# The recurrence's bias as one bfloat16 matmul, the roots' first guess as three-operand operations, and state weights loaded one stage earlier

## The chip, the cores and the metric

The kernel runs on 1 core of a Trainium2 chip. The metric is the device time of one execution, in microseconds (us); the median of several runs is compared. A core has five engines that run side by side, each through its own list of instructions in a fixed order: TensorE (PE, matmuls, with its weight loads PEld), VectorE (DVE), ScalarE (ACT), GpSimd (POOL) and SyncE (SP, which in this kernel issues most of the DMAs).

## The reference, cut to what matters

Two layers work on x (64 rows of batch × 64 steps × 256 channels) with a condition vector of 64 × 256. Layer 0: a conditioned decay scan, an attention, a modulated linear map, a ternary-weight feed-forward block. Layer 1: a tanh recurrence, a selective state-space block (mamba), a mixture of experts, a second mixture of experts. Each attention and feed-forward part adds to x. The change touches two of these parts and the weights of a third:

```python
# L0 ffn: two bitlinear layers (256 -> 1024 -> 256) with a squared relu between them
def bitlinear(x, norm_w, w):
    v = mean(square(x), axis=-1)                    # per row
    x_norm = x * rsqrt(v + 1e-8) * norm_w
    scale = 127 / clip(max(abs(x_norm), axis=-1), 1e-5)
    x_q = clip(round(x_norm * scale), -128, 127) / scale
    return einsum('bsd,hd->bsh', x_q, ternary(w))
h = act_scale * square(relu(bitlinear(x, norm1_w, w1))) + act_bias
y = bitlinear(h, norm2_w, w2)

# L1 cond: 64 steps, one after the other, on the x that layer 0 leaves
h = tanh(h @ Wh + x_t @ Wx + b)

# L1 attn: mamba, which reads its own weights W_in, W_xproj, W_dt, A_log, ...
```

## The kernel before, in words

**Stages.** One program runs the parts one after the other, with some overlap. By the trace: the conditioned scan (0 to about 152 us), the attention (about 153 to 383), the ternary feed-forward block with the recurrence woven into it (383 to 660), the rest of the recurrence (660 to 677), the head of the mamba block (677 to 722), its loop (to about 1700), and the two mixtures. A scheduler puts each engine's instructions into an order when the kernel is built, from dependences and its own costs, so the order of the source is only roughly that of the engines; no order is written out by hand here except that the matmuls of the recurrence carry a token that keeps them in their own order.

**The feed-forward block** (`ffn0`) works on x transposed, [256 channels, 4096 tokens], in 16 pairs of 256 tokens (`PT` = 4 steps of 64 rows, as `T` = 2 tiles of 128 tokens). A pair passes through nine stages, spread over `depth` = 7 turns, so that a turn of the loop (L726 to L738) does one stage for each of several pairs; 23 turns in all. Per turn:

- `product`: POOL scales x by the condition (L654), PE multiplies (L661), DVE scales the result (L663), ACT takes the sums of squares (L592).
- `weighted`: multiplies by the norm's weights, for 256 channels on POOL (L626), for 1024 on DVE (L628), then DVE finds the largest magnitude (L629).
- `roots_of` (L594 to L614): 1/sqrt(mean + EPS) for the 256-wide norm of one pair and the 1024-wide norm of another, on tiles of 128 × 2 or 128 × 4. DVE forms mean + EPS (L601, two instructions) and a first guess from the bits of the number taken as an integer (L602); then eleven instructions on POOL refine it and form the limit of the scale (L604 to L614).
- `rounded`: DVE inverts the magnitude (L637), takes the lesser of the scale and its limit (L638, which reads what L614 wrote), rounds (L645 on ACT for 1024, L647 on DVE for 256; L649 on DVE for both).
- `turn`, `up`, `turn_back`, `down`: transposes and matmuls on PE (L677, L688, L705, L713, L717), copies and relu on ACT, the square on DVE (L691) and the addition to x on DVE (L719).

**The recurrence** (`rnn`, L761 to L814) is a generator from which each turn from the 7th on takes four steps. Ahead of each four steps, `ahead` puts b + x_t·Wx for the four steps into a PSUM tile: for each of the two halves `o` of the output a bias matmul (L775: a fp32 row of the bias times a row of ones, one partition, 256 columns) and two fp32 matmuls with Wx (L786). Each step is four fp32 matmuls with Wh (L804) and one tanh on ACT (L813), whose result the next step's matmuls read. When the 23 turns are over, the feed-forward block stores x (L740) and the steps that are left run alone.

**The weights of the mamba block** (`mamba_weights`, L817 to L839; ten DMAs on SP) are asked for after the feed-forward block, in the room on chip that its weights leave (L2064 to L2066). A_log is then turned into -exp(A_log) in its own tile (L860 on ACT, L861 on DVE). The head (L892) multiplies the recurrence's output with `Win` (L902, PE) and starts the convolution (L906 on ACT, L909 on DVE).

**Earlier pieces that the change moves.** The scales of the ternary weights need the mean magnitude of w1 and w2 (L517, a DVE reduction over 2048 columns for each); the sums for the modulation use temporaries `ysq`, `wsq`, `d2` (`ffn0_prepared`). These pieces are put beside the conditioned scan and the attention. The conditioned scan works in chunks on DVE and ACT (L94 to L100 in the helper `softplus`, L199, L220).

Of the kernel before, what the change touches and what calls it, by code (L numbers as in the profile page):

```python
# [13 lines left out]
F32 = mybir.dt.float32  # L14
BF16 = mybir.dt.bfloat16
I32 = mybir.dt.int32
AF = mybir.ActivationFunctionType
ALU = mybir.AluOpType
# [3 lines left out]
P = 128  # L22
B, L, D = 64, 64, 256
# [3 lines left out]
KD = D // P  # L27
CB = CH // L
NTT = NT // P
EPS = 1e-8  # L30
# [7 lines left out]
def setup(ctx, tc, a):  # L38

    nc = tc.nc  # L40
    g = SimpleNamespace(nc=nc, tc=tc, a=a)
    const = ctx.enter_context(tc.tile_pool(name="const", bufs=1))
    g.ident = const.tile([P, P], F32, name="ident")
    make_identity(nc, g.ident)
    g.identb = const.tile([P, P], BF16, name="identb")
    make_identity(nc, g.identb)
    g.ones = const.tile([P, 1], F32, name="one")
    nc.vector.memset(g.ones, 1.0)
    g.magic = const.tile([P, 1], F32, name="magic")
    nc.vector.memset(g.magic, MAGIC)  # L50
    g.condT = const.tile([P, KD, B], F32, name="condT")
    nc.sync.dma_start(g.condT, a["condT"].rearrange("(k p) b -> p k b", p=P))
    g.x = tc.dram_tile((D, NT), F32, name="x_mid").rearrange("(k p) t -> p k t", p=P)
    return g
# [476 lines left out]
    return wq, s[:, 0:1], pieces()  # L531


def ffn0_prepared(g, pool, w):

    nc = g.nc
    w.ones = ones = pool.tile([P, P], F32, name="ones")
    nc.gpsimd.memset(ones, 1.0)
    n = KD * w.F // 2
    w.room = room = pool.tile([P, 2 * n], F32, name="room")  # L540
    w.w1q, w.m1, one = ternary(g, pool, w.w1, ones, "w1", room[:, :n])
    w.w2q, w.m2, two = ternary(g, pool, w.w2, ones, "w2", room[:, n:])

    w.ys = ys = pool.tile([P, KD, B], F32, name="ys")
    ysq = pool.tile([P, KD, 2, B], F32, name="ysq")
    wsq = pool.tile([P, KD, D], F32, name="wsq")
    w.d = d = pool.tile([P, D], F32, name="d")
    d2 = pool.tile([P, 2, D], F32, name="d2")

    def squares():  # L550
        nc.vector.tensor_scalar(ys, g.condT, 1.0 / math.sqrt(D), None, ALU.mult)
        for j in range(2):
            nc.vector.tensor_mul(ysq[:, :, j, :], ys, ys)
        nc.vector.tensor_mul(wsq, w.Wc, w.Wc)

    def sums():
        ps = bank(g)
        for k in range(KD):
            nc.tensor.matmul(
                ps[:, :D], ysq[:, k].rearrange("p j b -> p (j b)"), wsq[:, k, :], start=(k == 0), stop=(k == KD - 1)  # L560
            )
        nc.vector.tensor_scalar(d2[:, 0, :], ps[:, :D], EPS, None, ALU.add)

    return chain(one, two, (squares, sums)), (lambda: rsqrt(nc, d2[:, 0, :], d, d2[:, 1, :]),)


def ffn0(g, w, steps):

# [2 lines left out]
    nc, tc = g.nc, g.tc  # L573
# [7 lines left out]
    with (  # L581
# [12 lines left out]
        def roots_of(turn_, which):  # L594


            st = roots[turn_] = p3.tile([P, 4, 2, T], F32, name="roots")
            v, r, y, u = (st[:, i, which, :] for i in range(4))
            ss = sums.pop(turn_)
            for i, n in ((0, D), (1, F))[which]:  # L600
                nc.vector.tensor_scalar(st[:, 0, i, :], ss[:, i, :], 1.0 / n, EPS, ALU.mult, ALU.add)  # L601
            nc.vector.tensor_scalar(r.bitcast(I32), v.bitcast(I32), -0.5, 1597463007.0, ALU.mult, ALU.add)  # L602
            gp = nc.gpsimd
            gp.tensor_mul(y, r, r)  # L604
            gp.tensor_mul(y, y, v)
            gp.tensor_scalar(u, y, 0.375, -1.25, ALU.mult, ALU.add)
            gp.tensor_mul(u, u, y)
            gp.tensor_scalar(u, u, 1.875, None, ALU.add)
            gp.tensor_mul(r, r, u)
            gp.tensor_mul(y, r, r)  # L610
            gp.tensor_mul(y, y, v)
            gp.tensor_scalar(y, y, -0.5, 1.5, ALU.mult, ALU.add)
            gp.tensor_mul(r, r, y)
            gp.tensor_scalar(u, r, 127.0 / 1e-5, None, ALU.mult)  # L614
# [107 lines left out]
        depth = 7  # L722
        pairs = [SimpleNamespace() for _ in range(NP)]
        for turn_ in range(NP + depth):
            which = slice(0 if turn_ < NP else 1, 2 if 0 <= turn_ - 3 < NP else 1)
            if which.start < which.stop:  # L726
                sums[turn_] = p2.tile([P, 2, T], F32, name="ss")
            more = islice(steps, PT if turn_ >= depth else 0)
            for i, (stage, late) in enumerate(stages):
                if i % 2 == 0:  # L730
                    next(more, None)
                p = turn_ - late
                if 0 <= p < NP:
                    stage(p, pairs[p], turn_)
            if which.start < which.stop:
                roots_of(turn_, which)
            for _ in more:
                pass  # L738
# [8 lines left out]
def rnn_weights(g, pool):  # L747
    nc, a = g.nc, g.a
    w = SimpleNamespace()
    w.Wx = pool.tile([P, KD, D], F32, name="Wx")  # L750
    nc.sync.dma_start(w.Wx, a["rnn_Wx"].rearrange("(k p) n -> p k n", p=P))
    w.Wh = pool.tile([P, KD, D], F32, name="Wh")
    nc.sync.dma_start(w.Wh, a["rnn_Wh"].rearrange("(k p) n -> p k n", p=P))
    w.brow = pool.tile([1, D], F32, name="rb")
    nc.sync.dma_start(w.brow, a["rnn_b"].unsqueeze(0))
    w.one = pool.tile([1, 4 * B], F32, name="one")
    nc.vector.memset(w.one, 1.0)
    return w

# [85 lines left out]
def mamba(g, w, hs, beside):  # L845
# [3 lines left out]
    nc, tc = g.nc, g.tc  # L849
    NI, S, R = w.NI, w.S, w.R  # L850
# [4 lines left out]
    PI = 2  # L855
# [1 line left out]
    LEFT = 40  # L857
    BESIDE = 56
    BESIDE_LAST = 72
    nc.scalar.activation(w.A, w.A, AF.Exp)  # L860
    nc.vector.tensor_scalar(w.A, w.A, -1.0, None, ALU.mult)  # L861
    hs2 = hs.rearrange("p k b t -> p k (b t)")
    seq = lambda t: t.rearrange("p (b l) -> p b l", l=L)
    with (
# [3 lines left out]
        tc.tile_pool(name="m5", bufs=5) as p5,  # L868
        tc.tile_pool(name="mps", bufs=1, space=PSUM) as pp,
    ):  # L870
        tags = cycle(("mp", "yp0", "yp1", "cb"))
        one = lambda: pp.tile([P, CH], F32, tag=next(tags), name="mp")
        g.psum, g.tag = pp, "mq"
# [14 lines left out]
        for i in range(3):  # L888
            r = slice(i * 32, i * 32 + S)
# [140 lines left out]
        def decay(s):  # L1030
            c, j = divmod(s, STEPS)
            p, n = divmod(j, S)
            decays[s] = [dAs[(s * PI + i) % len(dAs)] for i in range(PI)]
            for i in range(PI):
                nc.scalar.activation(  # L1035
                    decays[s][i][:, :, 1:],
                    seq(vs[c].delta[p][:, i, :])[:, :, 1:],
                    AF.Exp,
                    scale=w.A[:, p * PI + i, n : n + 1],
                )  # L1040

        for _ in head(0, vs[0]):
# [4 lines left out]
        for s in range(AHEAD):  # L1047
            inputs(s)
        decay(0)
        cb = spread_c(vs[0], 0)  # L1050
        urgent, pieces, others = iter(()), iter(()), iter(())
        mid = None
        for s in range(LAST):
            c, j = divmod(s, STEPS)
            p, n = divmod(j, S)
            now = vs[c]
            if j == 0:
                ahead = head(c + 1, vs[c + 1]) if c + 1 < NCH else iter(())
                pieces = chain(pieces, gates(c, now, 0), islice(ahead, 2 * NI + 1), gates(c, now, PI), ahead)
# [959 lines left out]
def scoped(tc, name, side=None, bufs=1):  # L2019

    stack = ExitStack()
    kw = {"side": side} if side else {}
    return stack.enter_context(tc.tile_pool(name=name, bufs=bufs, **kw)), stack.close
# [3 lines left out]
def tile_adaln_attn_ffn_d2(ctx: ExitStack, tc: tile.TileContext, a: dict, out: bass.AP):  # L2027
    g = setup(ctx, tc, a)
    close_banks = banks(g)
    p_fill, close_fill = scoped(tc, "fill")  # L2030
    p_mid, close_mid = scoped(tc, "w_mid")
    p_x, close_x = scoped(tc, "x")
    p_attn, close_attn = scoped(tc, "w_attn")
    p_raw, close_raw = scoped(tc, "w_raw", side="right")
    w_attn = None

    def loads():
        nonlocal w_attn
        w_scan = scan_weights(g, p_attn)
        w_attn = attention_loads(g, p_attn, p_raw)  # L2040
        residual(g, p_x)
        g.nc.sync.dma_start(w_attn.Wout, a["WoutT"].rearrange("(k p) n -> p k n", p=P))
        return w_scan
# [6 lines left out]
    w_ffn0 = ffn0_weights(g, p_mid)  # L2050
    w_rnn = rnn_weights(g, p_mid)
# [1 line left out]
    weights = packed(g)  # L2053
    p_mix, close_mix = scoped(tc, "w_mix", side="right")
    p_hs, close_hs = scoped(tc, "hs", side="right")
    p_ffn0, close_ffn0 = scoped(tc, "w_ffn0", side="right")
    hs = p_hs.tile([P, KD, B, L], F32, name="hs")
    pieces = ffn0_prepared(g, p_ffn0, w_ffn0)
    spare = hs.rearrange("p k b t -> p (k b t)")
    attention(g, w_attn, cs, pieces, close_banks, spare, w_ffn0.room, w_ffn0.ones)  # L2060
    close_attn()
    with tc.tile_pool(name="steps", bufs=2, space=PSUM) as g.steps, tc.tile_pool(name="psum3", bufs=3, space=PSUM) as g.psum:
        ffn0(g, w_ffn0, rnn(g, w_rnn, hs))
    close_ffn0()  # L2064
    p_mamba, close_mamba = scoped(tc, "w_mamba", side="right")
    w_mamba = mamba_weights(g, p_mamba)  # L2066
    close_x()
    close_mid()
    p_shared, close_shared = scoped(tc, "w_shared", side="right")
# [93 lines left out]
```

## Time and profile before

| what | us |
|---|---|
| runs | 2809.3, 2803.34, 2809.07 |
| median | 2809.07 |
| the profiled execution | 2806.4 |
| its span (first to last instruction) | 2804.7 |
| PE busy in the span | 2368.8 (84%) |
| DVE busy | 1783.4 (64%) |
| ACT busy | 1380.3 (49%) |
| POOL busy | 1323.8 (47%) |

The profiled execution lies 1.7 us above its own span (what lies around it) and 2.7 us below the median of the three runs. The mean granted TensorE clock over the span is 0.924. Lines of the timeline give the start, the duration, the engine, the line of the kernel, the operation, what it writes and reads, and in brackets how long the engine had been idle and what released it. A group's line gives the sum of the busy time, the mean in ns, and the idle time ahead of it. A line of the table of windows gives, for a stretch of time, its length, the busy time of PE, PEld, DVE, ACT and POOL with the count of instructions, the granted clock, the share of the DMA engines, and GB/s.

### The profile page before, as it was taken

The page shows a single profiled execution, that of the slowest core. Times are in us where ns is not written, and L with a number is a line of the kernel's source. Part 1 is how long each engine was busy: PE and PEld are TensorE (multiplying, and loading weights), DVE is VectorE, ACT ScalarE, POOL GpSimd, SP SyncE. Part 2 cuts the span into 40 slices and gives each one's busy share as a digit, 9 for nine tenths or more (in the row PEclk, how much of TensorE's full clock was granted, in tenths as well). Part 3 has the DMA queues.
Part 4 walks back from the last instruction along what each step waited for, and adds up shares of the span by engine and source line. Part 5 has one row for each costly group of instructions (what it writes and reads, how often), then busy time and mean ns, then how long its engine had stood idle before and what let it go on. Part 6 is the DMA issues. An engine that isn't in the chain of part 4 may idle for free.

```text
span 2804.7 us, 34605 instructions
## 1 busy us (share of the span) xinstructions
PE 2368.8 (84%) x12072; PEld 1698.5 (61%) x12092; DVE 1783.4 (64%) x3017; ACT 1380.3 (49%) x2278; POOL 1323.8 (47%) x1158
## 2 busy tenths in 40 slices
PE   3979967998577888888778888869987999999995
PEld 3634435775245555555555555557765778888885
DVE  0467638982699889897978889883354443333332
ACT  0567627783675757676565757543332222222220
POOL 0013336540677676767586878754647341111110
PEclk9879988998768999998899899889999999999997
DMA  9999810002212122212122131314787757555545
GB/s 228 371 359 346 272 45 1 1 1 100 68 61 83 65 73 71 72 65 72 45 71 95 58 102 65 110 42 152 252 269 262 294 202 265 193 194 215 199 167 185
DMA packets 180630, 406.05 MB, mean 145 GB/s; under 512 B 24913, under 2 KB 84562, under 8 KB 175074
## 3 DMA queue, kind: packets, MB, share of 16 engines
q1 hardware_dynamic: 167010, 366.80, 38.7%
q0 software_dynamic: 13440, 36.98, 3.4%
q8 instruction: 97, 1.59, 0.2%
q14 instruction: 83, 0.68, 0.1%
HBM read 280.76 MB, written 144.98 MB: 152 GB/s over the span
## 4 chain that ended last, share of the span: by engine, by line
PE 45%; DVE 25%; issue 8%; ACT 7%; POOL 5%; DMA 3%; SPq 0%; DVEq 0%; POOLq 0%; ACTq 0%
DVE hb L1067 12%; PE ps L1661 11%; PE acc L1559 8%; PE out L446 4%; DVE hb L1069 3%; PE yp L1083 2%; PE mq L1797 2%; PE ps L1628 2%; PE mp L964 2%; DVE xc L909 2%; PE mq L1813 1%; PE acc L437 1%; PE s L412 1%; DVE h L628 1%; PE ps L1669 1%
## 5 line engine op out<-in xcount | busy, mean ns | idle before, releaser
L1028 POOL TENSOR_TENSOR hb<-dx,Bn 128x1024 f32<-128x1024 f32 x256 | 601.3, 2358 | 257.7 <-PE yp L1083 253.3
L1067 DVE TENSOR_TENSOR_SCAN hb<-dA,hb 128x512 f32<-128x512 f32 x512 | 602.5, 1208 | 32.4 <-ACT dA L1035 29.9
L1035 ACT ACTIVATE dA<-delta,A 128x504 f32<-128x504 f32 x512 | 344.4, 683 | 305.3 <-DVE hb L1067 302.7
L1083 PEld LDWEIGHTS yp<-ident,hb 128*128 128x128 f32 x2048 | 272.5, 154 | 179.2 <-issue 141.2
L1069 DVE TENSOR_TENSOR hb<-hb,cb 128x1024 f32<-128x1024 f32 x256 | 312.0, 1219 | 77.0 <-PE cb L980 59.5
L1661 PE MATMUL ps<-gxT,w 128*128 128x256 f32 (+1 forms) x1600 | 324.1, 361 | 0.8 <-DVE gxT L1536 0.8
L1083 PE MATMUL yp<-ident,hb 128*128 128x128 f32 x2048 | 307.6, 295 | 0.0
L1661 PEld LDWEIGHTS ps<-gxT,w 128*128 128x128 f32 x1600 | 276.4, 190 | 46.3 <-issue 12.4
L1797 PE MATMUL mq<-x,moe_s 128*128 128x256 f32 x896 | 254.6, 417 | 47.0 <-ACT up L1804 25.6
L1335 POOL DMA_INDIRECT ffn_y<-gy,to x72 | 69.2, 961 | 428.8 <-ACT gy L1561 416.3
L1797 PEld LDWEIGHTS mq<-x,moe_s 128*128 128x128 f32 x896 | 171.4, 207 | 109.8 <-ACT up L1804 34.1
L1665 DVE TENSOR_TENSOR gh<-gs,ps 128x256 f32<-128x256 f32 (+1 forms) x200 | 78.5, 393 | 205.3 <-ACT gs L1664 205.3
L980 PE MATMUL cb<-parts,pick 80*128 80x512 bf16 x256 | 106.5, 416 | 111.3 <-DVE hb L1069 96.5
L1559 PE MATMUL acc<-w,gh 128*128 128x256 f32 (+1 forms) x864 | 188.2, 388 | 0.0
L1664 ACT ACTIVATE gs<-ps 128x256 f32<-128x256 f32 (+1 forms) x200 | 72.4, 362 | 230.2 <-PE ps L1661 227.6
L1561 ACT ACTIVATE gy<-acc,wt 128x256 f32<-128x256 f32 x152 | 67.0, 472 | 234.1 <-PE acc L1559 229.6
L1559 PEld LDWEIGHTS acc<-w,gh 128*128 128x128 f32 (+1 forms) x864 | 145.4, 189 | 30.1 <-issue 13.4
L428 POOL TENSOR_TENSOR E<-E,z 128x1024 f32<-128x1024 f32 x32 | 61.6, 1924 | 151.9 <-DVE z L427 61.5
L446 PE MATMUL out<-oT,hs 128*128 128x512 f32 x256 | 119.5, 611 | 1.5 <-ACT oT L439 1.5
L1813 PE MATMUL mq<-moe_s,sh 128*128 128x256 f32 x448 | 114.3, 393 | 6.6 <-ACT up L1804 6.6
L1335 POOL DMA_INDIRECT moe_y<-gy,to x80 | 77.3, 966 | 68.2 <-ACT gy L1561 50.9
L1813 PEld LDWEIGHTS mq<-moe_s,sh 128*128 128x128 f32 x448 | 82.5, 194 | 40.5 <-issue 19.1
(459 smaller groups left out, 4376.6 us busy)
## 6 DMA issues: line engine op xcount, KB each, us to landing
w<-ffn_w SPq DMA_DIRECT2D x40, 2176.0 KB, 9.4
Bn<-B SPq DMA_DIRECT2D x128, 512.0 KB, 3.7
moe_x<-fill SPq DMA_DIRECT2D x130, 260.0 KB, 5.9
ffn_x<-fill SPq DMA_DIRECT2D x129, 260.0 KB, 6.0
w<-moe_w SPq DMA_DIRECT2D x48, 512.0 KB, 4.7
ffn_w<-in_ffn_W_dram SPq DMA_DIRECT2D x16, 640.0 KB, 8.3
gx<-moe_x SPq DMA_DIRECT2D x32, 260.0 KB, 5.0
gx<-ffn_x SPq DMA_DIRECT2D x32, 260.0 KB, 9.2
```

The source lines that it names most:

```text
L446: nc.tensor.matmul(ps, M[:, o, ts(k, P)], v.o[:, o], start=(o == 0), stop=(o == H // 2 - 1))
L980: nc.tensor.matmul(t, pick[:, n : n + 1].to_broadcast([rows, P]), v.parts, start=True, stop=True)
L1028: nc.gpsimd.tensor_mul(hb, vs[c].dx[p], Bn[:, n % NB, :].unsqueeze(1).to_broadcast([P, PI, CH]))
L1035: nc.scalar.activation(decays[s][i][:, :, 1:], seq(vs[c].delta[p][:, i, :])[:, :, 1:], AF.Exp, scale=w.A[:, p * PI + i, n : n + 1],)
L1067: ins = nc.vector.tensor_tensor_scan(h, dA[i].rearrange("p b l -> p (b l)"), h, 0.0, ALU.mult, ALU.add)
L1069: ins = nc.vector.tensor_tensor(hb, hb, cb.unsqueeze(1).to_broadcast([P, PI, CH]), ALU.mult)
L1083: nc.tensor.matmul(yp[i][:, t, :], hb[:, i, ts(t, P)], g.ident, start=(n == 0 and t == 0), stop=(n == S - 1 and t == CH // P - 1), is_tran ...
L1335: i = self.g.nc.gpsimd.indirect_dma_start(out=self.y, out_offset=bass.IndirectOffsetOnAxis(ap=to, axis=0), in_=y, in_offset=None)
L1559: nc.tensor.matmul(po[s], h, w, start=(i == 0), stop=(i == n - 1))
L1661: nc.tensor.matmul(ps[:, j, :], v.w12[:, k, ts(j * (full + 1) + i, P)], v.xT[:, k, :], start=(k == 0), stop=(k == KD - 1))
L1797: nc.tensor.matmul(ps[:, i % 2, :], w[:, k, ts(i, P)], xu[:, k, :], start=(k == 0), stop=(k == KD - 1))
L1813: nc.tensor.matmul(ps[:, t, :], h[:, i, ts(t, P)], self.s2[:, i, :], start=(i == 0), stop=(i == NS - 1))
```

## The change

Three edits that don't depend on each other.

1. In `roots_of`, mean + EPS (L601) and the first guess (L602) become `scalar_tensor_tensor` instructions: the constants EPS and 1597463007 are no longer immediates, they are read from two small constant tiles in SBUF (`g.eps`, 128 × 2, `g.guess`, 128 × 4), filled once at the start.
2. The recurrence's bias: the fp32 row is split into three bfloat16 parts (the rounded row, the rounded rest, the rounded rest of that), put at partitions 0, 32 and 64 of a zeroed tile of 65 partitions; the ones are a bfloat16 tile of 65 partitions. The matmul of L775 contracts over the 65 partitions in bfloat16. Splitting takes one more memset and eight small DVE operations, once.
3. The mamba weights are asked for at turn 7 of the feed-forward block. For that, the block's own weights move to the left side of the on-chip room, temporaries get a pool of their own that is closed after the attention, and -exp(A_log) goes to a new tile.

```diff
+    g.eps = const.tile([P, 2], F32, name="eps")
+    nc.vector.memset(g.eps, EPS)
+    g.guess = const.tile([P, 4], F32, name="guess")
+    nc.vector.memset(g.guess, 1597463007.0)
...
             for i, n in ((0, D), (1, F))[which]:
-                nc.vector.tensor_scalar(st[:, 0, i, :], ss[:, i, :], 1.0 / n, EPS, ALU.mult, ALU.add)
-            nc.vector.tensor_scalar(r.bitcast(I32), v.bitcast(I32), -0.5, 1597463007.0, ALU.mult, ALU.add)
+                nc.vector.scalar_tensor_tensor(st[:, 0, i, :], ss[:, i, :], 1.0 / n, g.eps, ALU.mult, ALU.add)
+            flat = lambda t: t.rearrange("p i t -> p (i t)")
+            first = g.guess[:, : flat(v).shape[1]]
+            nc.vector.scalar_tensor_tensor(flat(r).bitcast(I32), flat(v).bitcast(I32), -0.5, first, ALU.mult, ALU.add)
...
             more = islice(steps, PT if turn_ >= depth else 0)
+            if turn_ == depth:
+                loads()
...
-    w.brow = pool.tile([1, D], F32, name="rb")
-    nc.sync.dma_start(w.brow, a["rnn_b"].unsqueeze(0))
-    w.one = pool.tile([1, 4 * B], F32, name="one")
+    row = pool.tile([1, D], F32, name="rb")
+    nc.sync.dma_start(row, a["rnn_b"].unsqueeze(0))
+    part = pool.tile([1, D], BF16, name="rbp")
+    w.brow = pool.tile([65, D], BF16, name="rb3")
+    nc.vector.memset(w.brow, 0.0)
+    for i in range(3):
+        nc.vector.tensor_copy(part, row)
+        nc.vector.tensor_copy(w.brow[32 * i : 32 * i + 1, :], part)
+        if i < 2:
+            nc.vector.tensor_sub(row, row, part)
+    w.one = pool.tile([65, 4 * B], BF16, name="one")
...
-    nc.scalar.activation(w.A, w.A, AF.Exp)
-    nc.vector.tensor_scalar(w.A, w.A, -1.0, None, ALU.mult)
+        A = p1.tile([P, NI, S], F32, name="negA")
+        nc.scalar.activation(A, w.A, AF.Exp)
+        nc.vector.tensor_scalar(A, A, -1.0, None, ALU.mult)
...
-    pieces = ffn0_prepared(g, p_ffn0, w_ffn0)
+    p_temp, close_temp = scoped(tc, "temp", side="right")
+    pieces = ffn0_prepared(g, p_ffn0, p_temp, w_ffn0)
...
     close_attn()
+    p_mamba, close_mamba = scoped(tc, "w_mamba", side="right")
+    def loads_mamba():
+        nonlocal w_mamba
+        w_mamba = mamba_weights(g, p_mamba)
+    steps = rnn(g, w_rnn, hs)
     with tc.tile_pool(name="steps", bufs=2, space=PSUM) as g.steps, tc.tile_pool(name="psum3", bufs=3, space=PSUM) as g.psum:
-        ffn0(g, w_ffn0, rnn(g, w_rnn, hs))
+        ffn0(g, w_ffn0, steps, loads_mamba)
     close_ffn0()
-    p_mamba, close_mamba = scoped(tc, "w_mamba", side="right")
-    w_mamba = mamba_weights(g, p_mamba)
```

More of the change, by code (lines that the diff above doesn't have):

```diff
@@ L531, in ternary, with ffn0_prepared @@
     return wq, s[:, 0:1], pieces()
-def ffn0_prepared(g, pool, w):
+def ffn0_prepared(g, pool, temp, w):
     nc = g.nc
@@ L544, in ffn0_prepared @@
     w.ys = ys = pool.tile([P, KD, B], F32, name="ys")
-    ysq = pool.tile([P, KD, 2, B], F32, name="ysq")
-    wsq = pool.tile([P, KD, D], F32, name="wsq")
+    ysq = temp.tile([P, KD, 2, B], F32, name="ysq")
+    wsq = temp.tile([P, KD, D], F32, name="wsq")
     w.d = d = pool.tile([P, D], F32, name="d")
-    d2 = pool.tile([P, 2, D], F32, name="d2")
+    d2 = temp.tile([P, 2, D], F32, name="d2")
     def squares():
@@ L564, in ffn0_prepared, with ffn0 @@
     return chain(one, two, (squares, sums)), (lambda: rsqrt(nc, d2[:, 0, :], d, d2[:, 1, :]),)
-def ffn0(g, w, steps):
+def ffn0(g, w, steps, loads):
     nc, tc = g.nc, g.tc
@@ L1038, in decay @@
                     AF.Exp,
-                    scale=w.A[:, p * PI + i, n : n + 1],
+                    scale=A[:, p * PI + i, n : n + 1],
                 )
@@ L2032, in tile_adaln_attn_ffn_d2 @@
     p_x, close_x = scoped(tc, "x")
+    p_ffn0, close_ffn0 = scoped(tc, "w_ffn0")
     p_attn, close_attn = scoped(tc, "w_attn")
@@ L2055, in tile_adaln_attn_ffn_d2 @@
     p_hs, close_hs = scoped(tc, "hs", side="right")
-    p_ffn0, close_ffn0 = scoped(tc, "w_ffn0", side="right")
     hs = p_hs.tile([P, KD, B, L], F32, name="hs")
-    pieces = ffn0_prepared(g, p_ffn0, w_ffn0)
+    p_temp, close_temp = scoped(tc, "temp", side="right")
+    pieces = ffn0_prepared(g, p_ffn0, p_temp, w_ffn0)
     spare = hs.rearrange("p k b t -> p (k b t)")
     attention(g, w_attn, cs, pieces, close_banks, spare, w_ffn0.room, w_ffn0.ones)
+    close_temp()
     close_attn()
+    p_mamba, close_mamba = scoped(tc, "w_mamba", side="right")
+    w_mamba = None
+    def loads_mamba():
+        nonlocal w_mamba
+        w_mamba = mamba_weights(g, p_mamba)
+    steps = rnn(g, w_rnn, hs)
     with tc.tile_pool(name="steps", bufs=2, space=PSUM) as g.steps, tc.tile_pool(name="psum3", bufs=3, space=PSUM) as g.psum:
-        ffn0(g, w_ffn0, rnn(g, w_rnn, hs))
+        ffn0(g, w_ffn0, steps, loads_mamba)
     close_ffn0()
-    p_mamba, close_mamba = scoped(tc, "w_mamba", side="right")
-    w_mamba = mamba_weights(g, p_mamba)
     close_x()
```

## The prediction, made before the changed kernel ran

> **What bounds the kernel now.** I read the windows first, since the change touches one stage: the feed-forward block with the recurrence woven in (383 to 660 us) and the tail of the recurrence (to 677). Columns: window, its length, busy PE, PEld, DVE, ACT, POOL, granted clock, DMA share, GB/s.
>
> ```profile
> 460.00:600.00 140.00, 130.04 (x907) 102.59 (x920) 130.25 (x166) 111.81 (x215) 78.51 (x153) 0.99 0.00 1
> 600.00:660.00 60.00, 57.78 (x439) 47.14 (x440) 37.53 (x47) 43.25 (x74) 15.51 (x60) 1.00 0.04 12
> 660.00:677.00 17.00, 14.96 (x54) 11.34 (x53) 0.05 (x1) 1.92 (x5) 1.11 (x5) 0.52 0.92 314
> ```
>
> PE and DVE are equally busy from 460 to 600; from 600 PE alone is full; from 660 PE runs the last steps at half clock. Which of the two sets the pace to 600? In VectorE's timeline L628, once a turn, starts at 459.10 and nine turns later at 594.44: 15.04 us a turn. Now a turn in detail:
>
> ```profile
> 582.01 1.24 DVE L601 TENSOR_SCALAR roots<-ss 128x2 f32<-128x2 f32 x1
> 583.17 2.27 DVE L629 TENSOR_REDUCE st<-h 128x2 f32<-128x2048 f32 x1
> 585.37 1.21 DVE L649 TENSOR_SCALAR q<-h 128x2048 bf16<-128x2048 f32 x1
> 586.50 0.16 DVE L602 TENSOR_SCALAR roots<-roots 128x4 int32<-128x4 int32 x1
> ...
> 590.88 0.23 DVE L638 SCALAR_TENSOR_TENSOR st<-st,roots 128x2 f32<-128x2 f32 x2 [1.11 <-POOL roots L614]
> ```
>
> L601 on 128x2 takes 1.24 here, 0.17 where nothing is in its way (579.68). Its group, 383 to 660, then POOL at the same moment:
>
> ```profile
> L601 DVE TENSOR_SCALAR roots<-ss 128x2 f32<-128x2 f32 x32 | 21.8, 682 | 3.7 <-ACT junk L592 3.7
> ```
>
> ```profile
> 581.84 1.40 POOL L626 TENSOR_TENSOR gm<-gm,n 128x512 f32<-128x512 f32 x1 [4.57 <-ACT junk L592]
> ...
> 586.74 0.20 POOL L604 TENSOR_TENSOR roots<-roots 128x4 f32<-128x4 f32 x1 [3.50 <-DVE roots L602]
> ...
> 588.46 1.23 POOL L610 TENSOR_TENSOR roots<-roots 128x4 f32<-128x4 f32 x1
> ```
>
> L601 is long exactly while L626 (or L654, 1.5 us) runs on POOL. So DVE, not PE, sets these turns: about 12.0 us of work and 3.0 of stalls (1.1 at L601 under L626, 1.1 under L654, some 0.9 at L638 for POOL's roots). L638's waits come to 8.3 us in nine turns. From 600 the chain of waits lies wholly on PE:
>
> ```profile
> 605.40 0.62 PE steps L775 x2
> 606.03 1.06 PE steps L786 x4
> 607.09 0.62 PE steps L775 x2
> 607.71 1.06 PE steps L786 x4
> ```
>
> **What the Trainium skill says.** (1) "SBUF — State Buffer", section "Who interferes with whom": VectorE and GpSimd share one pair of ports, held for a whole instruction; VectorE contends when it has two SBUF inputs or a two-port mode. The trace agrees for the two-port candidate (L601: 0.17 or 1.24). (2) "VectorE: DVE Perf Modes", section "Mode 2×_2P — use both read ports for one tensor": with a second tensor operand that mode isn't available. So the three-operand form leaves the mode, but both its inputs are in SBUF, which by (1) contends as well. The trace agrees: L628, an operation of this kind, took 3.44 at 489.51 beside L626 (489.53, 1.27) and 2.35 at 579.75; POOL's L610 took 1.23 above, not 0.20, under the three-operand L691 at 588.37. (3) "TensorE: Matmul & The Clock Gate", section "Weight-path perf modes — Fast Weight Load (FWL) and DoubleRow": 128 weights that aren't fp32 load about twice as fast. The trace: 95 to 98 ns in bfloat16, 186 to 190 in fp32.
>
> **Part 1, the roots.** The instructions stay as many, of like size: L601, L602, L638 run in 0.15 to 0.17 unhindered, and L638 is already a three-operand one on 128x2. By the above I take the lock to stay on L601 at about 1.1; bounds: gone (−16.8 us over the 32 instances: 21.8 less 32 × 0.157), or the guess is caught too (+1.1 a turn). What does move is the order: built, the changed program has the guess ahead of L629 on 128x2048 in the turns of one parity and near it in the other, where L602 now comes after it. POOL's chain of eleven (about 3.1 us) then starts up to 2.2 us sooner, and L638's wait of 0.8 to 1.1 falls away or to 0.2. I walked both orders with the durations above, L601 blocked under L626 and L654, the guess under L654 where they meet: 14.2 and 14.95 a turn, mean 14.6, against 15.14 in turns with both POOL multiplies. Seven turns × 0.54 = 3.8; two turns without L654 at 1.2 = 2.4; about 1 before 460, where L638 waits longer (12.5 us) but DVE is busy 51 of 77 us and others set the pace. Sum −7. Bounds of this term: 0 (the next stall, ACT's sums, takes the place) and −15 (below). The cover ends at PE: its work in a turn is some 14.3 us, 13.3 after part 2, so a DVE turn of 14.6 stays the later one, PE's idle time between.
>
> **Part 2, the bias.** A bias matmul shows two records, 0.62 us per half; bfloat16 matmuls of 256 columns run 8 in 0.87 (L713), 0.11 each, with a weight load 0.09 shorter. Saved per half 0.42 to 0.51, take 0.475; per `ahead` 0.95. Sixteen run, but those up to 600 lie beside DVE's work. On the chain are four: those that begin at 605.40, 616.56, 640.49, 651.50 (the one at 628 stands beside ACT): 4 × 0.95 = 3.8. The last, at half clock (660.57 and 663.64, 1.07 to 1.15 each), saves 1.6. Sum −5.4; bounds −2 (the steps' tanh on ACT is late next and eats the four) and −7. The split of the row: one memset and eight small DVE operations of about 0.3, once.
>
> **Part 3, the loads, and what moved with it.** Ten DMAs leave SP's place behind the block. Before, `Win` was issued at 656.59 and landed at 661.96, the last at 676.80. Who waits for them? PE's L902 starts at 677.26, released by POOL's L887, which follows
>
> ```profile
> 675.85 0.98 POOL L882 MEMSET parts<- 80x512 bf16 x2 [17.18 <-PE steps L804]
> ```
>
> that is, by the recurrence's end; ACT's L906 then waits for L902 and not for a DMA. All landed before they were needed: gain 0, bounds −2 and +1. In SP's new order the loads stand ahead of moe_s's and the stores L740; they wait for the attention's last matmuls (366, 382), nothing else is queued behind them until the stores at 659, and the DMA engines are idle to 660 (share 0.00): no cost. The stores landed up to 673.5, 2 us ahead of what now waits for the recurrence; they move up with the block and have the queue to themselves.
>
> The order on VectorE changes early: w1's reduction (L517, 2.28 us) goes between L98 and L100 of the scan's first chunk, w2's and most of the bias split after that chunk's L220, where before VectorE stood idle:
>
> ```profile
> 113.91 0.68 DVE L220 TENSOR_TENSOR cs<-t,s 128x512 f32<-128x512 f32 x1
> 119.34 0.48 DVE L199 TENSOR_SCALAR conv<-acc,conv_b 128x256 f32<-128x256 f32 x1 [4.75 <-ACT conv L196]
> ```
>
> 2.28 and six small operations of 0.3 fit 4.75; 2.28 against a gap of 1.94 to 2 does not quite. I take +0.4; bounds 0 and +7.0 (2 × 2.28 + 8 × 0.3, nothing hidden). From the mamba head on the orders are unchanged.
>
> **Sum**: −7 −5.4 +0 +0.4 = −12.0 on the profiled execution's 2806.4: 2794.4. The profiled execution stands 2.67 below the median of the runs; on the median 2809.07 − 12.0 = 2797.1.
>
> **Rivals.**
> A, the three-operand form escapes the lock. For: a mode is left. Against: L628 at 489.51. A DVE turn falls to some 13.4, PE's 13.3 next: 9 × (15.04 − 13.4) = 14.8, + 1 + 5.4 − 0.4 = 20.8: 2788.
> B, part 1 does nothing: another wait (ACT's L592, 0.43 ahead of L601 now, or the guess held under L654) takes over, and only PE's part is seen, in part. −5.4 to −1.6, +0.4, take −4: 2805. For: stalls in this stage pass from one to the next; against: L638's wait has no second releaser close behind.
> C, slower: VectorE's queue in the scan. It is in order; w1's reduction now stands amid the first chunk and waits for w1's DMA. Before, w1 and w2 had landed by 79 and the bias row by about 82, 25 us ahead; the DMA engines are full then (share 1.02 to 153). If w1 came only later than 109, every us of it would be added to the scan and all behind it. It decides from the point where the scan's last L220 (147.05 before) ends more than 12 us later; for slower than can be measured, 18. With landing at 127 the result is 2815. For: full queues; against: their order ahead of w1 is the same.
> That the change doesn't do what it says is A's converse: the locked L601 stays, which my main case contains.
>
> **Chances.** Main case 0.62 (2797, itself 2790 to 2804), A 0.15, B 0.16, C 0.07. 0.2% (5.6 us) is what a measurement of this kernel can tell from no change; below 2803.4 lie A and most of the main case, with a little of B: 0.75; within: 0.18; above: 0.07. The range 2785 to 2807 takes in A and most of B and leaves out C and the edges, about 0.16.
>
> **What would show it.** In the profile after: L601's successor still long (1.2) beside L626; the guess before L629 on h; L638's idle time for POOL's roots under 3 us in nine turns, not 8.3; L628's pitch 14.6; the bias records 0.11 to 0.2 a half; the scan's last L220 near 147.5; L902 about 12 us earlier than 677.26, still released by L887. A pitch of 13.4 with a short L601 shows A; one of 15 shows B; a late L220 shows C. I would be wrong on size most easily in the pitch.

## The result and the profile after

| | before | changed |
|---|---|---|
| median of 20 runs each, us | 2807.86 | 2800.86 |
| lowest to highest | 2798.76 to 2818.86 | 2788.64 to 2805.74 |
| profiled execution / its span | 2806.4 / 2804.7 | 2796.62 / 2794.9 |
| first L628 of the feed-forward block | 416.7 | 411.6 |
| recurrence ends (last tanh) | 676.2 | 656.0 |
| mamba's head (first matmul with Win) | 677.26 | 656.93 |

The ratio is 0.9976, 95% interval 0.9967 to 0.9985: 6.7 us faster (4.2 to 9.3) where 12 were forecast. The time lies in the range. But the traces don't show a gain of 12 that came out somewhat small: they show one of 20.3 us at the mamba's head, of which 9.8 are left at the end. Both numbers need a reason.

After the change line numbers are higher: L601 is L605, L602 L608, L626 L632, L628 L634, L638 L644, L775 L791, L804 L820. The windows of the changed kernel (columns as before):

```profile
460.00:600.00 140.00, 126.60 (x952) 105.18 (x953) 135.96 (x180) 115.88 (x221) 82.41 (x169) 0.98 0.00 1
600.00:660.00 60.00, 54.11 (x399) 46.05 (x397) 27.36 (x37) 34.52 (x62) 10.16 (x48) 0.90 0.19 71
```

VectorE is now clearly the fuller engine to 600. A turn of its timeline, and two of POOL's multiplies in it, which answer to the turn shown in the prediction:

```profile
500.09 1.23 DVE L605 SCALAR_TENSOR_TENSOR roots<-ss,eps 128x2 f32<-128x2 f32 x1
501.34 0.69 DVE L635 TENSOR_REDUCE st<-gm 128x2 f32<-128x512 f32 x1
501.94 1.22 DVE L655 TENSOR_SCALAR q<-h 128x2048 bf16<-128x2048 f32 x1
503.07 0.16 DVE L608 SCALAR_TENSOR_TENSOR roots<-roots,guess 128x4 int32<-128x4 int32 x1
503.15 2.28 DVE L635 TENSOR_REDUCE st<-h 128x2 f32<-128x2048 f32 x1
...
509.86 1.32 DVE L644 SCALAR_TENSOR_TENSOR st<-st,roots 128x2 f32<-128x2 f32 x1
```

```profile
498.41 2.89 POOL L632 TENSOR_TENSOR gm<-gm,n 128x512 f32<-128x512 f32 x1 [1.77 <-ACT junk L596]
...
509.64 1.52 POOL L660 TENSOR_TENSOR xs<-xT,ys 128x512 f32<-128x512 f32 x1
```

L605 on 128x2 still takes 1.23, to the end of L632: the three-operand form is held up just as the old one. The guess (503.07) now stands ahead of the long reduction (503.15), in two turns of three, so in nine turns L644 waits 1.0 us for POOL's roots. But L644 itself is now held up (1.32, beside L660). The groups of the stage, L638 of the kernel before first, then L605 and L644 of the changed one (busy us, mean ns, then the idle time ahead):

```profile
L638 DVE SCALAR_TENSOR_TENSOR st<-st,roots 128x2 f32<-128x2 f32 x32 | 4.0, 158 | 21.9 <-POOL roots L614 21.7
```

```profile
L605 DVE SCALAR_TENSOR_TENSOR roots<-ss,eps 128x2 f32<-128x2 f32 x32 | 20.8, 649 | 2.6 <-ACT junk L596 2.6
...
L644 DVE SCALAR_TENSOR_TENSOR st<-st,roots 128x2 f32<-128x2 f32 x32 | 8.2, 284 | 14.1 <-POOL roots L620 13.9
```

The idle time falls from 21.9 to 14.1 us, and L644 gives back 4.2 of that as a longer operation.

### The profile page after: what moved, and what is told of

Same layout as the page of the kernel before. It is cut to its first block, busy times and chain, and to the rows that moved or that the text cites. A ratio compares the mean times of both kernels' runs of the same rounds, so it can differ in the third digit from the quotient of the medians.

```text
span 2794.9 us, 34560 instructions
## 1 busy us (share of the span) xinstructions
PE 2350.0 (84%) x12060; PEld 1692.7 (61%) x12060; DVE 1787.2 (64%) x3028; ACT 1381.1 (49%) x2278; POOL 1327.4 (47%) x1158
## 4 chain that ended last, share of the span: by engine, by line
PE 46%; DVE 26%; issue 7%; ACT 6%; POOL 5%; DMA 4%; SPq 0%; DVEq 0%; POOLq 0%; ACTq 0%
DVE hb L1084 12%; PE ps L1678 11%; PE acc L1576 8%; PE out L450 4%; DVE hb L1086 3%; PE mq L1814 2%; PE yp L1100 2%; PE ps L1645 2%; PE mq L1830 2%; PE mp L981 2%; DVE xc L926 1%; POOL hb L1045 1%; DVE h L634 1%; PE mp L919 1%; PE s L416 1%
## 5 line engine op out<-in xcount | busy, mean ns | idle before, releaser
L1052 ACT ACTIVATE dA<-delta,negA 128x504 f32<-128x504 f32 x512 | 344.3, 683 | 308.2 <-DVE hb L1084 305.0
L1830 PEld LDWEIGHTS mq<-moe_s,sh 128*128 128x128 f32 x448 | 84.0, 197 | 42.5 <-issue 20.3
```

The lines of the kernel that those rows point to most:

```text
L1052: nc.scalar.activation(decays[s][i][:, :, 1:], seq(vs[c].delta[p][:, i, :])[:, :, 1:], AF.Exp, scale=A[:, p * PI + i, n : n + 1],)
L1830: nc.tensor.matmul(ps[:, t, :], h[:, i, ts(t, P)], self.s2[:, i, :], start=(i == 0), stop=(i == NS - 1))
```

## The experiments

All ratios are against the kernel before in the same set of runs, on the same chip. In two of the three sets after the first it took 2861 and 2852 us; the traces from there lose 40 to 54 us in the mixtures (1900 to 2320 us), whatever the edit, so these sets are compared by ratios and by the times at which stages begin. "Earlier there" is against 676.2 in the trace of the kernel before, one trace each; "faster in all" is the ratio times the median of before in its set. Both are in us, and a minus sign means later or slower.

| kernel | ratio [95%] | recurrence ends | earlier there | faster in all | first matmul of all |
|---|---|---|---|---|---|
| the change | 0.9976 [0.9967, 0.9985] | 656.0 | 20.2 | 6.7 | 24.41 |
| roots_only | 1.0021 [1.0008, 1.0035] | 686.3 | −10.1 | −6.0 | 27.83 |
| bias_only | 0.9940 [0.9921, 0.9959] | 660.7 | 15.5 | 17.2 | 24.50 |
| loads_only | 0.9997 [0.9985, 1.0010] | 678.9 | −2.7 | 0.9 | 27.84 |
| guess_first | 0.9963 [0.9948, 0.9978] | 664.4 | 11.8 | 10.6 | 24.31 |
| whole_again | 0.9969 [0.9959, 0.9980] | 655.5 | 20.7 | 8.7 | 24.50 |
| no_loads | 0.9997 [0.9989, 1.0005] | 671.6 | 4.6 | 0.8 | 27.61 |
| one_column | 0.9907 [0.9894, 0.9920] | 646.6 | 29.6 | 26.1 | 24.47 |
| idle_at_head | 1.0033 [1.0020, 1.0046] | 685.5 | −9.3 | −9.3 | 24.45 |
| idle_short | 0.9982 [0.9971, 0.9993] | 670.0 | 6.2 | 5.1 | 24.88 |
| one_column_alone | 0.9956 [0.9940, 0.9972] | 664.5 | 11.7 | 12.6 | 24.54 |
| no_loads_again | 0.9979 [0.9965, 0.9993] | 675.7 | 0.5 | 6.0 | 27.87 |
| column_and_order | 0.9912 [0.9894, 0.9931] | 648.9 | 27.3 | 25.1 | 24.39 |

**The parts alone.** The edits are those of the diff, one part at a time: part 1 (`g.eps`, `g.guess` in L601 and L602), part 2 (the bias in three bfloat16 parts), part 3 (loads and places).

> Part 1 alone (three-operand L601 and L602), all else as before. Built, its order on VectorE in the feed-forward block is that of before. Theory 1 (the three-operand form is held up as before, and it is the bias edit that moved the guess ahead of the reduction): no change, 0 us (-2 to +2), L601 still 0.65 us on the mean, L638 waits for POOL's roots as before (8 us from 460 to 600). Rival, as the prediction put it (part 1 carries the roots' gain): -7 us.

Measured: +0.21%, some 6 us slower. The order and the groups are as forecast (the trace of roots_only):

```profile
L605 DVE SCALAR_TENSOR_TENSOR roots<-ss,eps 128x2 f32<-128x2 f32 x32 | 22.3, 698 | 4.3 <-ACT junk L596 4.3
...
L644 DVE SCALAR_TENSOR_TENSOR st<-st,roots 128x2 f32<-128x2 f32 x32 | 4.1, 158 | 21.3 <-POOL roots L620 21.0
```

Nothing is gained by part 1. The loss is about a late start: the first matmul of the whole program comes 3.5 us late and the scan 6.9 us late, as the first DMAs on SP take longer to issue. Two other kernels have this too; see no_loads_again.

> Part 2 alone (bias as one bfloat16 matmul). Built, the guess now stands ahead of the reduction on h. Theory 1 (this edit holds both the order of the roots and TensorE's saving): the recurrence ends 13 to 16 us earlier than 676, the whole is 4 to 6 us faster, since a part is given back by the mamba's end. Rival, as the prediction put it (part 2 is worth TensorE's 5.4 us only): recurrence 5 us earlier, the whole -5.

Measured: −0.60% (0.41 to 0.79), more than either theory: 17 us. The guess is ahead of the reduction and the recurrence ends 15.5 us early, within what theory 1 gave. So the order came with the bias: the scheduler places the instructions of all engines together, and an edit of a matmul moved the roots on another engine. Whether the cheaper matmul did it or the small DVE operations that split the row, no run separates.

> Part 3 alone (mamba weights early, the block's weights on the left side). Built, the reductions of w1 and w2 (L517) stand in the scan as in the changed kernel. Theory 1 (the gain of 5.1 us at the attention comes from these reductions): the first L628 comes 5 us earlier than 416.7, the mamba's head the same 5, the whole -2 to -5. Rival, as the prediction put it: nothing gained, +0.4.

Measured: no change in all. It starts 7.0 us late like roots_only, and has made up 6.4 of that by 224 us; theory 1 holds for the stage, and both theories' times miss, by the late start. Most of it (4.3, between the scan's end and the attention's first matmul) is made up at a branch, which I had overlooked. In the kernel before (VectorE's timeline):

```profile
147.09 2.29 DVE L517 TENSOR_REDUCE w1s<-w 128x1 f32<-128x2048 f32 x1
149.29 2.27 DVE L517 TENSOR_REDUCE w2s<-w 128x1 f32<-128x2048 f32 x1
...
158.97 0.69 DVE L417 TENSOR_REDUCE mx<-s 128x8 f32<-128x512 f32 x1 [6.27 <-PE s L412]
```

and the first matmul of the attention, on PE, and the branch (`tc.If` at L336), on the engines' sequencers (ns, then the start in us):

```profile
156.79 1.98 PE L412 MATMUL s<-hs,k 64*64 64x256 f32 x16 [8.96 <-DVEq L336]
```

```profile
L336 POOLq COMPARE_BRANCH  x1: 45/45/45, 147.8 to 147.8; - x1
L336 PEldq COMPARE_BRANCH  x1: 3700/3700/3700, 147.9 to 147.9; - x1
...
L336 ACTq COMPARE_BRANCH  x1: 50/50/50, 148.5 to 148.5; - x1
...
L336 DVEq COMPARE_BRANCH  x1: 72/72/72, 152.7 to 152.7; - x1
L336 DVEq EVENT_SEMAPHORE  x1: 21/21/21, 156.6 to 156.6; - x1
```

These engines meet at the branch. POOL, PE and ACT reached it between 147.8 and 148.5, and PE's part of it took 3.7 us, to 151.6. VectorE arrived last, at 152.7, because the two reductions stood ahead of it, and only then, 3.9 us later, could it go on and did the attention begin. In the changed kernel the reductions are inside the scan and the attention's first matmul starts at 153.88.

> The kernel before with one order forced on VectorE: the guess (L602) ahead of the reduction L629 on h. Bias in fp32, loads late. Theory 1 (the order of the guess is what shortens VectorE's turns): pitch of L628 14.5 instead of 15.04, the wait of L638 for POOL's roots near 1 instead of 8.3 us, the recurrence ends 5 us earlier, the whole -2 to -4. Rival (the turns are shorter because TensorE's work is): pitch 15.0, no change.

```diff
+            ins = nc.vector.tensor_scalar(r.bitcast(I32), v.bitcast(I32), -0.5, 1597463007.0, ALU.mult, ALU.add)
+            g.tc.stamp_issue_order_token(ins.ins, "guess")
...
+            ins = nc.vector.tensor_reduce(am, x, AX.X, ALU.max, apply_absolute_value=True)
+            if n == F:
+                g.tc.stamp_issue_order_token(ins.ins, "guess")
```

Measured: −0.37% (0.22 to 0.52), recurrence 11.8 us early, pitch of L628 about 14.0. Theory 1 holds and was too small. With VectorE's other instructions nearly all in their old order from 460 us on, the place of this one shortens each turn by one us. With the token the guess stands ahead of the rounding of h as well, earlier still than in the changed kernel (pitch 14.5).

**Where the rest went.**

> The changed kernel itself, once more, beside its parts. Its trace stood 20 us ahead of before at the mamba's head and 10 at the end. Theory 1 (the stretches in which TensorE's granted clock falls come at much the same times whatever the program does, so a program that is shifted by 20 us meets them at other work: a gain or loss by chance of some 10 us): again about 20 us ahead at the head (start-up apart), the loss after it of another size or at other places than in the first trace; the whole -0.2% to -0.6%. Rival (the early loads or the new places in SBUF make the mamba loop itself slower): the same loss of 8 to 10 us between 1400 and 1750, the whole -0.24%.

Measured: −0.31%. The head is again 20.8 us early; this time the trace, that of its fastest execution, is 22.6 ahead at the end: nothing is lost. So the early loads and the new places in SBUF don't always make the loop slower, and one_column and column_and_order, which have them too, keep their lead to the end (see the table): the rival falls, as far as it is a loss that comes with the loads. The windows about where the first trace lost 2.7 us within 4 us of the loop (at 1411 of the kernel before), in the changed kernel, then in its second trace:

```profile
1380.00:1400.00 20.00, 17.57 (x71) 11.50 (x70) 16.09 (x16) 12.34 (x20) 11.20 (x6) 0.83 0.14 54
1400.00:1420.00 20.00, 18.15 (x71) 12.21 (x70) 15.23 (x15) 15.45 (x23) 16.45 (x7) 0.74 0.22 67
```

```profile
1380.00:1400.00 20.00, 18.38 (x93) 12.87 (x93) 18.83 (x18) 13.73 (x21) 14.49 (x7) 1.00 0.21 65
1400.00:1420.00 20.00, 15.61 (x74) 10.97 (x73) 16.90 (x17) 17.47 (x25) 17.80 (x9) 0.91 0.26 83
```

The granted clock is 0.83 and 0.74 where the same work ran at 1.00 and 0.91. Two further losses of the first trace, 3.4 us about 1565 and 2.4 about 1707 of the kernel before, also fall where its clock is low (0.74 and 0.74 from 1540 to 1580, 0.83 and 0.91 from 1680 to 1720; before 0.96, 0.84, 1.00, 1.00). Both traces are of executions faster than the median of their set (2796.6 against 2800.9, 2783.8 against 2798.8), so the median execution ends later than either, and of it there is no trace.

> The changed kernel with the last tanh of the recurrence repeated 63 times on ACT (same values written again), which keeps TensorE idle for about 17 us ahead of the mamba's head. The loop then runs at about the times of before. Theory 1 (what the loop loses depends on when the clock falls): the idle time costs less than its length, 5 to 12 us. Rival (an idle stretch on the chain costs its whole length): 16 to 18 us slower than the changed kernel.

> The changed kernel with the last tanh repeated 22 times instead of 63 (0.41 us each in the trace of the long one: 9.1 us of idle time for TensorE at the mamba's head). So far 26 us of it cost 17.0. Theory 1 (what is lost after the head depends on how the program lies against the falls of the clock): the cost isn't in proportion; 9 us cost -3 to +4. Rival A (a fixed share of every microsecond is given back, 17 of 26): +6. Rival B (idle time on the chain costs its length): +9.

```diff
-            nc.scalar.activation(hs[:, :, :, t], now[:, :, t - t0, :], AF.Tanh)
+            for _ in range(64 if t == L - 1 else 1):
+                nc.scalar.activation(hs[:, :, :, t], now[:, :, t - t0, :], AF.Tanh)
```

(The short one has 23 in place of 64.) A repeat takes 0.414 us, so the idle time was 26.1 us (not 17, as the first expectation had it) and 9.1. Against the changed kernel the long one costs 17.0 us on the medians (ratios: 18, about 13 to 23): more than the 5 to 12 of theory 1, near the rival's number only because the rival's length was wrong, and clearly less than its length. The short one came from another chip; by the ratios it costs 0.0013 ± 0.0015, some 3.6 us (−0.6 to +7.8). That leaves out its full length, and it can't tell theory 1 from a constant share (some 6 us).

That looks as if a microsecond at the mamba's head were less than one at the end. The table says otherwise. Against the kernel before, the long one is 9.3 us late at the recurrence's end and 9.3 in all, the short one 6.2 early and 5.1. In the eleven rows other than the change and whole_again the two columns lie within 6 us of each other, and in eight of them the first lies inside the interval of the second. Only the changed kernel loses more, both times: 20.2 and 20.7 us at the recurrence's end, 6.7 and 8.7 in all. So the cost of the idle time looks small because the kernel that it is compared with has this loss. Why that one kernel gives back 12 to 14 us, when with single columns it gives back 3.5 and without part 3 at most 3.8, stays open.

**The size of part 3, and the start.**

> The change without part 3: the mamba weights late, the reductions of w1 and w2 behind the scan as before. Theory 1: the attention 5 us later than in the changed kernel, the recurrence's end 15 us ahead of before; the whole -0.4% to -0.6%, as with the bias alone. Rival (part 3 costs in the loop what it gains in the attention): faster than the changed kernel by 5 us or more.

> The changed kernel without part 3 once more, for one reading: its first matmul of L168 began at 27.6 us in its trace instead of 24.3, and the scan 6.7 us late, since the first DMAs on SP took 17% longer to issue. Theory (it belongs to the kernel as built and laid out, since three of ten traces have it and the times of this kernel hold together): 27.6 again. Rival (it belongs to the single execution or loading): 24.3 this time and the whole 5 us faster than last time against before.

Measured: −0.03% and −0.21%; the recurrence ends 4.6 us early and, the late start of 6.9 taken off, 11.5 (0.5 and 7.8 in the second trace). Against the changed kernel on the same chip it is 8.7 us slower, not faster: the rival falls. The difference is less than the branch (theory 1's 5 us) and the late start are worth together, since the changed kernel gives back more behind the recurrence. Theory 1's number for the whole misses mainly by that start; in the first of the two it falls short even with 6.9 us added (0.27% for 0.4%). The repeat settled the start: 27.87 us again, on another chip, so it goes with the kernel as built; the two traces of the changed kernel agree in the same way (24.4 and 24.5). Of the kernels traced, roots_only, loads_only and no_loads (twice) have it, with the first matmul at 27.6 to 27.9; the others, before and the changed one too, begin at 24.3 to 24.9. Why the three are laid out so that SP takes 11.8 instead of 10.1 us to issue the scan's first transfers wasn't found.

**The stall itself.**

> The changed kernel with L605 as single-column operations with immediates (four on 128x1 instead of two on 128x2; same values). Theory 1 (VectorE is held up in L605 by POOL because the operation takes two streams from SBUF or is read in two halves, which one element cannot be): each takes about 0.15 us beside POOL's L632 and L660 too, L605's group falls from 20.8 us to 10 for 64, the pitch of L628 falls from 14.5 to 13.5, and the recurrence ends 5 to 9 us earlier. Rival (POOL blocks any operation of VectorE on small tiles): the group's mean stays above 0.4 us, no gain. The stall may also go to the next operation that reads SBUF twice, L634 or L644: then the pitch stays at 14.5.

> The kernel before with L601 as four single-column operations with immediates, all else as before: bias in fp32, loads late. Theory 1 (VectorE sets the turns by its stalls beside POOL, and TensorE with its 14.3 us a turn is next): pitch of L628 14.2 to 14.5 instead of 15.04, recurrence's end 5 to 8 us ahead, the whole -4 to -8; each L601 0.14 us. Rival (the gain of the single columns comes from the order, not from the port): L601 stays long, no gain.

```diff
-                nc.vector.scalar_tensor_tensor(st[:, 0, i, :], ss[:, i, :], 1.0 / n, g.eps, ALU.mult, ALU.add)
+                for j in range(T):
+                    nc.vector.tensor_scalar(st[:, 0, i, j : j + 1], ss[:, i, j : j + 1], 1.0 / n, EPS, ALU.mult, ALU.add)
```

one_column: −0.93% (0.80 to 1.06), 27.6 us on the medians, the best of all. (Alone, the line that goes is L601 with its immediates.) Its group and, beside POOL's two multiplies, one instance:

```profile
L606 DVE TENSOR_SCALAR roots<-ss 128x1 f32<-128x1 f32 x64 | 7.9, 139 | 6.6 <-ACT junk L596 6.6
```

```profile
495.68 1.74 DVE L656 TENSOR_SCALAR q<-gm 128x512 bf16<-128x512 f32 x1
497.34 0.20 DVE L606 TENSOR_SCALAR roots<-ss 128x1 f32<-128x1 f32 x2
497.46 2.27 DVE L636 TENSOR_REDUCE st<-h 128x2 f32<-128x2048 f32 x1
```

```profile
493.61 3.53 POOL L661 TENSOR_TENSOR xs<-xT,ys 128x512 f32<-128x512 f32 x1
497.09 1.46 POOL L633 TENSOR_TENSOR gm<-gm,n 128x512 f32<-128x512 f32 x1
```

At 497.34 POOL's L633 has just begun, and two single-column operations go through in 0.20 where L601 waited 1.24. Theory 1 holds: most turns take 13.57. And here the guess stands behind the long reduction in every turn, so the gain isn't one of order. VectorE is still the fuller engine (busy 137.1 us of the 140 from 450 to 590, TensorE 128.7). A stall remains: the rounding L656 on 128x512 now takes 1200 ns on the mean, L649 on the same tile took 646 in the kernel before. The recurrence ends 8.9 us earlier than in whole_again, the whole 19 us earlier on the medians; the other 10 are the loss behind the recurrence, most of which this kernel doesn't have. On the kernel before alone the same edit gives −0.44% and 11.7 us at the recurrence's end, more than the 5 to 8 expected; there the 64 single-column instances take 142 ns, and the guess keeps its old place, so the rival falls.

> The changed kernel with single columns in L605 and the guess forced ahead of the reduction on h, a candidate for the best. If the wait of L644 for POOL's roots (11.6 us in all with single columns alone) still bears on the chain: 2 to 4 us faster than single columns alone, -1.1% on before. If TensorE (13.3 us of 13.6 in a turn) is the bound already: the same as single columns alone, -0.9%.

Measured: −0.88% (0.69 to 1.06), pitch 14.38, recurrence's end 648.9 against 646.6: no gain on single columns alone. That is the second number, but not for its reason: the turn is 0.8 us longer than without the forced order, not held at TensorE's bound. The order takes one wait away and brings another, since the reduction on the product (L637 on gm) now stands ahead of the guess and waits for POOL's multiply L634, 13.9 us in the stage, where in one_column it waited 4.6.

## Why the prediction was right, and where it wasn't

**The lock on L601** was right: 20.8 us for 32 instances after, 21.8 before, and roots_only shows it without the other parts (22.3). The Trainium skill, "SBUF — State Buffer", section "Who interferes with whom", says that an operation with two inputs in SBUF contends with GpSimd, and L628 in the trace of before had shown it. Rival A is out.

**The roots' order** was right in size: pitch from L628 at 452.6 to 583.1 is 14.50 against 14.6 forecast; L644 waits 1.0 us for POOL in nine turns, not 8.3. Between 386 and 594 of the kernel before the lead grows from 5.1 to 11.4 us: 6.3, with 7 forecast from 383 to 600. It was booked to the wrong edit. The prediction called it part 1's, since it happens to the roots; roots_only keeps the old order, bias_only has the new one. The floor that the prediction set under the turns was too high: guess_first, with the old bias, runs them in 14.04 us, under the 14.3 that TensorE was said to need.

**The bias** was forecast at 5.4 us. The bias of a half takes 0.12 instead of 0.62, as assumed, but the two matmuls with Wx behind it (L802, L786 before) take less time as well. In the changed kernel:

```profile
639.95 0.29 PE L791 MATMUL steps<-one,rb 65*128 65x256 bf16 x1
640.08 1.03 PE L802 MATMUL steps<-xT,Wx 128*128 128x256 f32 x4
640.94 0.27 PE L791 MATMUL steps<-one,rb 65*128 65x256 bf16 x1
```

From start to start a half takes 0.99, and it took 1.69 (605.40 to 607.09 in the prediction): 0.70 saved, where the prediction took 0.475. And from step 49 to the last the recurrence takes 42.4 us before and 35.1 after: 7.3, and all kernels with the old bias take 42 to 43, those with the new 34 to 36.5. Two `ahead` at full clock and the one of the tail lie in that stretch, for which the prediction had 2 × 0.95 + 1.6 = 3.5. Six halves at 0.70 are 4.2; the other 3 or so go with the clock. The last 16 us in the kernel before, then in guess_first, which still has the fp32 bias, then in bias_only:

```profile
660.20:676.20 16.00, 14.17 (x48) 10.83 (x47) 0.00 (x0) 1.91 (x5) 0.35 (x1) 0.51 0.95 326
```

```profile
648.40:664.40 16.00, 14.14 (x50) 10.89 (x49) 0.00 (x0) 1.92 (x5) 0.38 (x1) 0.53 0.95 329
```

```profile
644.70:660.70 16.00, 13.40 (x95) 11.60 (x92) 1.38 (x3) 3.94 (x10) 1.84 (x7) 0.98 0.72 266
```

Half clock was taken as a given of the tail; with the new bias most of it is gone from there. It isn't gone altogether: in the 26 us ahead of that last window bias_only runs at 0.86 and 0.87, where the kernel before runs at 1.00. By length and clock the kernel before misses 7.8 us of full clock in these 42 us, the changed one 3.8.

**The loads** were right on what they are for: no transfer was on the path, and loads_only ends the recurrence's tail with no gain. They were wrong on what comes with them. The prediction saw that w1's and w2's reductions moved, and asked only what they would cost in the scan; what their leaving gives at their old place it put at nothing, without a reason. The 6.27 us of VectorE's idle time behind them hold the branch at which all others had waited for VectorE. The scan paid 1.7 us (last L220 at 146.36, then 148.12; 0.4 forecast, within its bounds), the branch gave 4.7 (from 1.76 late to 2.91 early), and a further 2.2 came by 205 us, with a clock of 0.80 and 0.93 where it had been 0.71 and 0.65.

**The sum**: 20.3 us at the mamba's head, not 12. A head that is early was then taken to be an end that is as early, because the orders from there on are unchanged. That holds, within some us, for the eleven other kernels and repeats, and failed for this one: 9.8 left in one trace, 22.6 in the other, 6.7 and 8.7 over all executions. So part 2 alone (17.2 by its ratio) is worth more than the three parts together, though its recurrence ends 5 us later than theirs. That the loss goes with the granted clock in the loop is what the windows of one trace show; what sets that clock, and why the median execution loses more, isn't settled. That the clock falls at the same times whatever runs, which was my theory, doesn't hold for the tail, where the fall moved with the recurrence's end, from 676 to 664 us in guess_first. So the forecast of 2797 came near by luck: two errors of opposite sign, one of 8 and one of some 14 us.

## What to carry to other kernels

Ask of idle time what released it, a branch or another engine's wait included: work ahead of a meeting point is paid by all, however idle its engine is afterwards. A short operation that is long only beside another engine's is a stall to be taken away, here by an operation on one element a partition instead of two; on the kernel before it was worth 12.6 us (8 to 17), where the whole change was worth 6.7 and 8.7. And try each edit alone: a scheduler can move another engine's work for it, and here one part alone was faster than all three. Before a loss is taken for a rule, set each kernel against the same base: here it was the loss of a single kernel.

## What the runs showed of the hardware that was not expected

- One-element operations escape the stall: 139 ns on the mean in 64 instances, where 128x2 took 682 (immediates) and 649 (three operands). This agrees with the Trainium skill, "VectorE: DVE Perf Modes", section "Mode 2×_2P — use both read ports for one tensor", by which the mode gives each of two ports one half of the outermost dimension longer than one: a tile of one element a partition has none to halve. That this is the reason is argued; that single elements are free of POOL is shown by the three kernels that have them (139 to 143 ns on the mean).
- The last 16 us of the recurrence ran at a granted clock of 0.50 to 0.55 in all five kernels with the fp32 bias (before, roots_only, loads_only, guess_first, one_column_alone), at 0.74 to 0.98 in the seven traces with the bfloat16 one that have no idle time put in. The Trainium skill, "TensorE: Matmul & The Clock Gate", section "What's actually happening", has a clock that recent activity sets to half or full. The windows of 0.50 and 1.00 agree with the two levels. That activity sets them no run here shows: PE was busy 14.1 to 14.2 of the 16 us in the two windows of low clock above, and 13.4 in that of 0.98. That the low clock goes with the old bias is shown by the pairs; whether it is fp32, the single partition or the order of the work, which changed too, isn't.
- In three of the kernels SP took 11.7 to 11.8 us for each of the scan's first large transfers instead of 10.1, on two chips, and the scan came some 7 us late.
